# Two-layer graph network on one Trainium2 core: PSUM of the second linear map split into two groups of banks, two more pairs of half-batches in seven products, and the loads, copies and normalization steps around them reordered

## Chip, cores and metric

The kernel runs on one core of one Trainium2 chip, all in fp32. The metric is the device time of one execution in microseconds; a kernel's time is the median of its runs. Times inside an execution come from the hardware profiler.

## What is computed

The input is x of 16 batches (B) with 1024 nodes (N) and 256 channels (C), and one matrix adj of 1024x1024. In short:

```python
# layer 0
h = relu(layernorm(x))                              # per node
Wg = adj * A(column means of h)                     # a matrix per batch, from a sigmoid of differences
g = relu((h^T @ Wg) * para);  q = g^T in 4 heads
k, v = (h @ kv_w) in 4 heads
x = x + softmax(q k^T * scale) v
# layer 1
h = relu(layernorm(x))
agg = A_hat @ h                                     # A_hat from adj, once
z1 = agg @ W1^T + b1                                # 256 -> 512 (the first map)
h = relu(batchnorm(z1))                             # statistics over all 16*1024 nodes
z2 = h @ W2^T + b2                                  # 512 -> 256 (the second map)
x = x + batchnorm(z2)                               # again over all nodes
```

Both batch norms need their statistics over all nodes before anything behind them can start. So z1 is written to memory and read back, and z2 is kept in SBUF until it is complete.

## The kernel before

**Engines and order.** TensorE (PE in the profile) multiplies, VectorE (DVE) and ScalarE (ACT) do the element work and the copies out of PSUM, GpSimd (POOL) a few small steps and the turning of h by DMA, SyncE (SP) issues most loads and stores. Inside `tc.manual_schedule` the order of instructions on each engine is the order in which the program calls them; what an engine waits for follows from the tiles. A tile pool hands out buffers in turn; a request waits until the buffer's last reader is done. A DMA is issued by an engine's queue in order, so a load that waits for its buffer holds back the DMAs behind it on that queue.

**Stage 1** loops over the batches: attention of batch b, with the graph step of batch b+1 and the first map of earlier work placed between. `graph(b, between)` (L374) forms g, then queries, values (L423) and keys; at fixed places it calls the steps that the caller hands it in `between`. `between[7]` is `norm.relu(4, NC)`: `norm` is the layer-1 layer norm of the other batch, and its relu (L278) is done on ScalarE chunk by chunk, eight chunks of 128x256, each 0.505 us apart. Keys of b of 2 and more are formed as seven products of 2x2 blocks (Strassen's scheme in Winograd's form) with one PSUM bank `x` that goes on accumulating: after each step ScalarE copies it out (L474, L478, L482, L487). `between[8]` calls `leave` (stores x, L927) and `arrive(b + 2)`, which loads x of a coming batch on SyncE (L188) into the one buffer from which the relu reads.

`linear1` (L672) multiplies by A_hat (L690) in seven products, from four sums of parts of h that VectorE makes (L683 to L686); `linear1_seven` (L781) does the map W1 in seven products (L796), with `store` and `stats` (bn_stats, L835) of its results. Batches 14 and 15 run at the end of the stage (L1157 to L1189). There the step `third` turns W2 by TensorE into a PSUM tile of 128x1024 of the pool `ps_s` (L1027), and ScalarE copies it out (L1176).

**Stage 2** (from L1192) treats 32 half-batches t of 512 nodes. t of 31 and 30 and their z1 are the last to come out of stage 1, and their relus are done in place. A plain half-batch takes 8 matmuls of 128x512 (L1221): four pieces of 128 features, two output blocks c. `Pair(p)` (L1251) does the half-batches 2p and 2p+1 together in seven products of two matmuls (L1283), 14 in place of 16, in the order m1, m2, m6, m7, m5, m3, m4. m1, m6, m5 and m3 go on accumulating in the bank `x` (f_zx), which `keep` copies out by ScalarE after each (L1294); m2, m7 and m4 go to other banks (f_zm), which VectorE adds to z2 (L1297). VectorE makes the sums t1 to t4 of the relus (L1273, L1274, L1278, L1279). ScalarE applies the batch norm and relu of z1 in place (L152), after the loads (L163). m1 of pair p+1 stands between m5 and m3 of pair p.

All of these banks come from one pool `ps_z` of 8. The half-batches 0 and 1 are done plain at the start (begun with two of the four pieces, since those norms are ready first), the pairs 1 to 12 in seven products, the half-batches 26 to 29 plain, and 30 and 31 at the end in a pool `ps_last` of four banks (L1473). Plain results are copied to z2 by VectorE (L1349). Each result's statistics are a bn_stats on VectorE (L1234).

Then come the second batch norm and the **output** loop over b (L1512 to L1555): `finish` scales z2 (L1498 on ScalarE, L1500 on VectorE), TensorE turns it back (L1516, f_outps), VectorE adds it to x (L1549), and ScalarE's queue stores it (L1550). x is loaded again by `load_x1` (L1205) into tiles of the pool `io`, ten batches ahead at most. That pool also serves the loads of z1 for the pairs; it has 15 tiles of 512 KB.

Of the kernel before, what the change touches and what calls it, by code (L numbers as in the profile page):

```python
# [29 lines left out]
def fast_path(  # L30
# [140 lines left out]
    with ExitStack() as stage:  # L171
# [202 lines left out]
        def graph(b, between):  # L374
# [43 lines left out]
            def values():  # L418
                for c4 in range(0, NC, 4):
# [10 lines left out]
                    nc.scalar.copy(v[:, c4 : c4 + 4, :], ps)  # L430

            if b < 2:
                for d in range(CC):
                    ps = ps_s.tile([P, N], F32, tag="s", name=f"f_kps_{b}_{d}")
                    for g in range(NH):
                        for e in range(CC):
                            nc.tensor.matmul(
                                ps[:, ts(g, 512)],
                                kvw_t[:, e, ts(d, P)],
                                hT[e][:, ts(g, 512)],  # L440
                                start=(e == 0),
                                stop=(e == CC - 1),
                            )
                    nc.scalar.copy(kT[:, d, :], ps)
                    queries(d)
                values()
                return qT, kT, v
# [27 lines left out]
            mult(m2, a(0, 1), part(1, 0))  # L475
            nc.vector.tensor_add(c(0, 0), c(0, 0), m2)
            mult(x, sums[:, 1], t2, True)
            nc.scalar.copy(c(1, 0), x)  # L478
            mult(m7, sums[:, 2], t3)
            nc.vector.tensor_add(c(1, 0), c(1, 0), m7)  # L480
# [190 lines left out]

        def linear1(b, h1, thirds, between):  # L672


            def a(i, k):
                return h1[:, KH * k : KH * (k + 1), ts(i, P)]

            def pair_of_sums(n):
                return pp.tile([P, 2, KH, P], F32, tag="acc", name=f"f_hs{n}_{b}", bufs=2)

            s12, s34 = pair_of_sums(1), pair_of_sums(3)
            s1, s2, s3, s4 = s12[:, 0], s12[:, 1], s34[:, 0], s34[:, 1]
            nc.vector.tensor_add(s1, a(1, 0), a(1, 1))  # L683
            nc.vector.tensor_sub(s2, s1, a(0, 0))  # L684
            nc.vector.tensor_sub(s3, a(0, 0), a(1, 0))
            nc.vector.tensor_sub(s4, a(0, 1), s2)  # L686

            def product(ps, left, right, more=False):
# [91 lines left out]

        def linear1_seven(b, agg, sums, up, middle):  # L781

# [81 lines left out]
            add_biased(0, 1, m3)  # L864
            store(0, 1)
            stats(1, 1)
            stats(0, 1)
# [24 lines left out]

        def linear1_all(b, h1, thirds, early, late, last):

# [8 lines left out]
            def second(agg, up):  # L903
                if up is None:
                    up = ow.tile([P, 2, 512], F32, tag="oT", name=f"f_u4_{b}", bufs=2)
                linear1_seven(b, agg, sums[0], up, last)

# [14 lines left out]

            linear1(b, h1, thirds, [first, late, second if b + 1 < B else very_last])

# [105 lines left out]
        with tc.manual_schedule(engines={ENG.PE, ENG.Activation, ENG.DVE, ENG.Pool, ENG.SP}):  # L1030
# [73 lines left out]
            for b in range(B):  # L1104
# [14 lines left out]
                def more(c):  # L1119
# [12 lines left out]
                    6: [lambda: norm.relu(0, 4)],  # L1132
                    7: [lambda: norm.relu(4, NC)],
                    8: [lambda: leave(b), lambda: arrive(b + 2)],
# [25 lines left out]
                else:  # L1160
# [11 lines left out]
                    def third():  # L1172
                        left[5]()
                        norm.stats(4, NC)
                        norm.invert()
                        nc.scalar.copy(  # L1176
                            w2T.rearrange("p f c -> p (f c)"), turned(w2n, CC, FC, "w2")
                        )
                        norm.relu(0, NC)
# [7 lines left out]

                    linear1_all(b - 1, kept_h, thirds, first, second, third)
                    linear1_all(b, norm.h, thirds, nothing, nothing, nothing)  # L1189


    with ExitStack() as stage:  # L1192
        big = stage.enter_context(tc.tile_pool(name="fbig2", bufs=1))
        io = stage.enter_context(tc.tile_pool(name="fio", bufs=NH * (AHEAD - 3) + 1))

# [13 lines left out]
        with tc.manual_schedule(engines={ENG.PE, ENG.Activation, ENG.DVE, ENG.Pool, ENG.SP}):  # L1209
            bn1.affine(FC - 2, FC)  # L1210

            z2 = big.tile([P, CC, B - 1, N], F32, tag="z2", name="f_z2")
            zps = ExitStack()
            ps_z = zps.enter_context(tc.tile_pool(name="fps_z", bufs=8, space=PSUM))

            def bank(name):
                return ps_z.tile([P, 512], F32, tag="z", name=name)

# [30 lines left out]
            class Pair:  # L1249
# [5 lines left out]
                def load(self):  # L1255
# [7 lines left out]
                    self.b[0, 0] = fetch(t0, 0, new("b11"))  # L1263
                    self.b[1, 0] = fetch(t0, 2)
                    self.b[0, 1] = fetch(t1, 0, new("b12"))
                    self.b[1, 1] = fetch(t1, 2, new("b22"))
                    self.t4 = new("t4")

# [30 lines left out]
                def m1(self):  # L1299
                    self.x = bank(f"f_zx_{self.p}")  # L1300
                    self.mult(self.x, a(0, 0), self.b[0, 0], True)
# [45 lines left out]
            def plain_out(t, ps):  # L1347
                for c in range(CC):
                    nc.vector.tensor_copy(place(t, c), ps[c])  # L1349
                    stats(t, c)  # L1350

            SEVEN = range(1, B - 3)
            rest = range(2 * SEVEN[-1] + 2, TT - 2)

            def fetch_all(t):
                for f2 in range(0, FC, 2):
                    z = io.tile([P, 2, 512], F32, tag="x1", name=f"f_zz_{t}_{f2}")
                    zs[t, f2] = fetch(t, f2, z)

# [4 lines left out]
            pairs = {p: Pair(p) for p in SEVEN}  # L1364
            begun = {}
            for t in range(2):
                begun[t] = [bank(f"f_z2ps_{t}_{c}") for c in range(CC)]
                plain(t, begun[t], 0)
            weight_sums()
            for t in range(2):  # L1370
                relu_on(zs[t, 2], 2)
                plain(t, begun[t], 2)
            first = pairs[SEVEN[0]]
            first.load()
            for k, j in ((0, 0), (0, 1), (1, 1), (1, 0)):
# [8 lines left out]
            for p in SEVEN:  # L1384
                now, soon = pairs[p], pairs.get(p + 1)
                if p + 2 in pairs:
                    pairs[p + 2].load()
                now.m2()
                stats(now.t[0], 0)
                if soon:  # L1390
                    soon.relu(0, 0)
                    soon.relu(0, 1)
                now.m6()
                now.keep(0, 1)
                now.m7()
                if soon:
                    soon.relu(1, 1)
                    soon.relu(1, 0)
                now.m5()
                now.keep(1, 1)  # L1400
                if soon:
                    soon.sums13()
                    soon.m1()
                    soon.keep(0, 0)
                else:
                    for t in rest:
                        fetch_all(t)
                    for t in range(TT - 2, TT):
                        for f2 in range(0, FC, 2):
                            zs[t, f2] = fetch(t, f2)  # L1410
                    for n in range(AHEAD - 3):
                        load_x1(n)
                    ps = [bank(f"f_z2ps_{rest[0]}_{c}") for c in range(CC)]
                    relu_all(rest[0])
                    plain(rest[0], ps, 0)
                now.out(1)
# [12 lines left out]
            load_x1(AHEAD - 1, [(lasting, "w2n", 1), (io, "x1", None)])  # L1429
            for n, t in enumerate(rest):  # L1430
                if n == 0:
                    plain(t, ps, 2)
                else:
                    ps = [bank(f"f_z2ps_{t}_{c}") for c in range(CC)]
                    relu_all(t)
                    plain(t, ps, 0)
                    plain(t, ps, 2)
                plain_out(t, ps)
            zps.close()
            ps_out = stage.enter_context(tc.tile_pool(name="fps_out", bufs=2, space=PSUM))  # L1440
            ps_last = stage.enter_context(tc.tile_pool(name="fps_last", bufs=4, space=PSUM))
            last = {}
            for t in range(TT - 2, TT):
                relu_all(t)

# [14 lines left out]
            for c in range(CC):  # L1460
                for t in range(TT - 2, TT):
                    ps = ps_last.tile([P, 512], F32, tag="last", name=f"f_z2ps_{t}_{c}")
                    last[t % 2, c] = ps
# [31 lines left out]
            def scaled(out, src, c, by_scalar):  # L1495
# [3 lines left out]
                else:  # L1499
                    nc.vector.tensor_scalar(out, src, s, t, ALU.mult, ALU.add)  # L1500

            def by_scalar(b, c):
                return c == 0 or b % 2 == 1

# [15 lines left out]
            for b in range(B):  # L1520
# [6 lines left out]
                if b == 0:  # L1527

                    finish(0, 0)
                    finish(1, 0)  # L1530
                    for h in range(NH):
# [8 lines left out]
                else:  # L1540
                    for h in range(NH):
                        for c in range(CC):
                            turn_out(b, h, c, outs[h])
                soon = [(b + 2, c) for c in range(CC)] if b + 2 < B else []
                for n in soon:
                    if by_scalar(*n):
                        finish(*n)
                for h in range(NH):
                    nc.vector.tensor_add(xt[h], xt[h], outs[h])  # L1549
                    nc.scalar.dma_start(out_v[:, 4 * h : 4 * h + 4, :], xt[h])  # L1550
                for n in soon:
                    if not by_scalar(*n):
                        finish(*n)
                if b + AHEAD < B:
# [515 lines left out]
```

## Time and profile before

| | us |
|---|---|
| runs | 2447.23, 2447.41, 2450.25 (median 2447.41) |
| profiled execution | 2446.91 |
| its span | 2445.0 |
| VectorE busy | 1777.3 (73%) |
| ScalarE busy | 1316.7 (54%) |
| start of stage 2's first matmul | 2169.44 |
| start of the output's first transposition | 2377.93 |
| last transposition | 2433.24 |

The granted TensorE clock was 0.996 of full speed. In a line of the timeline the first number is the start in us from the beginning of the span, the second the length of a group of instructions; then follow the engine, the line in the kernel, the operation, its output and inputs by the program's names, and how many instructions the group has. Brackets give the idle time of the engine just before, and what ended it. In the list of waits, the numbers are the total, how often, and the longest.

### The profile page before, as it was taken

What the parts mean: (1) busy time and instruction counts of PE and PEld (TensorE: products, weight loads), DVE (VectorE), ACT (ScalarE), POOL (GpSimd) and SP (SyncE); (2) the same over time, 40 slices, a digit from 0 to 9 for tenths busy, and PEclk for the clock granted to TensorE, in tenths of its full rate; (3) what the DMA queues carried; (4) which work ended last, traced back from release to release, by engine and by line L of the source; (5) the groups of instructions that cost most, each with busy time, mean ns of one, the idle gap of its engine ahead of it and who ended that gap; (6) DMA issues with size and microseconds to landing.
All of it is one profiled execution on the core that took longest, in us unless ns stands there. A gap on an engine that the chain in (4) does not pass through costs nothing.

```text
span 2445.0 us, 24677 instructions
## 1 busy us (share of the span) xinstructions
PE 2390.1 (98%) x8050; PEld 1052.2 (43%) x8050; DVE 1777.3 (73%) x2440; ACT 1316.7 (54%) x1918; POOL 308.2 (13%) x546
## 2 busy tenths in 40 slices
PE   8999999999999999999999999999999999999995
PEld 4443444434343434344443434343444434434444
DVE  6878677685959596776859595958777687747746
ACT  6845556454636464654546364645546465346633
POOL 2030202020110303020202002030202020000000
PEclk9999999999999999999999999999999999999998
DMA  5041414232322424141422233241414211455569
GB/s 185 9 139 61 151 61 142 69 109 68 109 86 75 128 64 148 61 151 61 125 78 90 79 100 103 67 144 61 151 61 138 74 49 51 142 194 172 167 214 377
DMA packets 176632, 275.76 MB, mean 113 GB/s; under 512 B 37872, under 2 KB 121328, under 8 KB 176496
## 3 DMA queue, kind: packets, MB, share of 16 engines
q1 hardware_dynamic: 156336, 241.55, 30.6%
q0 software_dynamic: 15552, 15.77, 2.5%
q10 hardware_dynamic: 4608, 16.78, 1.7%
q8 instruction: 66, 1.08, 0.2%
q14 instruction: 70, 0.57, 0.1%
HBM read 169.35 MB, written 71.10 MB: 98 GB/s over the span
## 4 chain that ended last, share of the span: by engine, by line
PE 79%; DVE 11%; SPq 3%; DMA 3%; ACT 2%; issue 2%; POOL 1%; DVEq 0%; ACTq 0%; POOLq 0%
PE f_aps L690 15%; PE f_s L501 14%; PE f_o L542 14%; PE f_gps L398 13%; PE f_zps L796 5%; DVE f_acc L518 3%; PE f_vps L423 3%; PE f_zx L1283 3%; SPq L606 3%; PE f_zm L1283 2%; PE f_kpsx L464 2%; PE f_z2ps L1221 2%; PE f_kps L464 1%; ACT f_h_b L278 1%; DVE f_w L349 1%
## 5 line engine op out<-in xcount | busy, mean ns | idle before, releaser
L509 ACT ACTIVATE f_p<-f_s 128x1024 f32<-128x1024 f32 x512 | 477.3, 1048 | 153.4 <-PE f_s L501 153.3
L518 DVE TENSOR_TENSOR f_acc<-f_acc,f_p 128x1024 f32<-128x1024 f32 x384 | 470.4, 1225 | 41.1 <-ACT f_p L509 0.5
L501 PE MATMUL f_s<-f_qT,f_kT 64*128 64x512 f32 x2048 | 456.8, 596 | 0.0
L542 PE MATMUL f_o<-f_p,f_v 128*64 128x512 f32 x2048 | 453.6, 595 | 0.0
L398 PE MATMUL f_gps<-f_w,f_h_a 128*128 128x512 f32 x1024 | 444.7, 594 | 0.3 <-DVE f_w L336 0.3
L368 POOL DMA_DIRECT2D f_hT<-f_hQ x480 | 235.8, 499 | 1219.9 <-PE f_gps L398 1170.7
L501 PEld LDWEIGHTS f_s<-f_qT,f_kT 64*128 64x128 f32 x2048 | 190.7, 185 | 263.6 <-ACT f_p L509 117.3
L398 PEld LDWEIGHTS f_gps<-f_w,f_h_a 128*128 128x128 f32 x1024 | 192.8, 190 | 247.0 <-issue 229.8
L542 PEld LDWEIGHTS f_o<-f_p,f_v 128*64 128x64 f32 x2048 | 141.4, 137 | 304.3 <-issue 253.9
L349 DVE SCALAR_TENSOR_TENSOR f_w<-f_w,f_adj 128x1024 f32<-128x1024 f32 x127 | 153.8, 1212 | 38.8 <-ACT f_w L348 38.8
L345 ACT ACTIVATE f_w<-f_row,f_col 128x1024 f32<-128x1024 f32 x127 | 147.0, 1158 | 28.1 <-DMA f_row<-frow 18.7
L278 ACT ACTIVATE f_h_b<-f_x,f_shift_b,f_rstd_b 128x256 f32<-128x256 f32 x128 | 64.7, 587 | 161.0 <-DVE f_shift_b L263 161.0
L348 ACT ACTIVATE f_w<-f_w 128x1024 f32<-128x1024 f32 x127 | 134.3, 1058 | 4.0
L690 PE MATMUL f_aps<-f_ahatT,f_hs 128*128 128x512 f32 x256 | 115.1, 592 | 0.0
L690 PE MATMUL f_aps<-f_t,f_hs 128*128 128x512 f32 x256 | 112.5, 592 | 1.3 <-DVE f_hs L684 1.3
L423 PE MATMUL f_vps<-f_kvw,f_hT 128*128 128x256 f32 x512 | 113.1, 379 | 0.0
L690 PE MATMUL f_aps<-f_ahatT,f_h_b 128*128 128x512 f32 x256 | 112.6, 592 | 0.0
L278 ACT ACTIVATE f_h_a<-f_x,f_shift_a,f_rstd_a 128x256 f32<-128x256 f32 x126 | 73.8, 587 | 63.4 <-DVE f_shift_a L263 63.4
L423 PEld LDWEIGHTS f_vps<-f_kvw,f_hT 128*128 128x128 f32 x512 | 97.3, 190 | 20.1 <-issue 7.4
L515 DVE TENSOR_TENSOR f_acc<-f_p,f_p 128x1024 f32<-128x1024 f32 x64 | 76.2, 1191 | 15.3 <-ACT f_p L509 15.3
L584 ACT COPY f_recs<-f_rec 32x32 f32<-32x32 f32 x128 | 31.5, 246 | 98.6 <-DVE f_rec L576 97.5
L569 ACT COPY f_parts<-f_red 32x64 f32<-32x64 f32 x128 | 39.1, 305 | 78.4 <-DVE f_red L534 77.3
(230 smaller groups left out, 2694.8 us busy)
## 6 DMA issues: line engine op xcount, KB each, us to landing
f_t<-ft SPq DMA_DIRECT2D x84, 512.0 KB, 6.9
fz<-f_z SPq DMA_DIRECT2D x64, 512.0 KB, 9.7
f_x<-in_x_dram SPq DMA_DIRECT2D x31, 1024.0 KB, 7.8
f_zb<-fz SPq DMA_DIRECT2D x36, 512.0 KB, 4.2
f_para<-in_L_gnn_para_dram SPq DMA_DIRECT2D x32, 512.0 KB, 4.4
f_att<-f_oT SPq DMA_DIRECT2D x512, 32.0 KB, 1.9
fx<-f_x SPq DMA_DIRECT2D x16, 1024.0 KB, 6.5
f_x1t<-fx SPq DMA_DIRECT2D x32, 512.0 KB, 6.6
```

The lines of the kernel that those rows point to most:

```text
L278: nc.scalar.activation(self.h[:, c, :], self.xt[:, c, :], AF.Relu, bias=self.shift[:, c : c + 1], scale=self.rstd[:, c : c + 1], accum_out ...
L345: nc.scalar.activation(w, rows[b], AF.Abs, bias=cols[b][:, c : c + 1], scale=0.5 / C)
L348: nc.scalar.activation(w, w, AF.Tanh)
L349: nc.vector.scalar_tensor_tensor(w, w, 1.0, adj_t[c], ALU.subtract, ALU.mult)
L368: queue.dma_start(to[ts(k, 32), ts(a, 32 * NC)], t[ts(a, 32), k].rearrange("i c r -> i (c r)"),)
L398: nc.tensor.matmul(gps[d][:, ts(g, 512)], hs[b][:, c, ts(d, P)], w[:, ts(g, 512)], start=(c == 0), stop=(c == NC - 1),)
L423: nc.tensor.matmul(ps[:, i, :], hT[e][:, ts(c4 + i, P)], kvw_t[:, e, C : 2 * C], start=(e == 0), stop=(e == CC - 1),)
L501: nc.tensor.matmul(ps[:, e, :], kT[rows_e, pair, ts(m, P)], qT[rows_e, pair, ts(g, 512)], start=True, stop=True,)
L509: nc.scalar.activation(p, ps, AF.Exp)
L518: nc.vector.tensor_add(acc_of[s], acc_of[s], p)
L542: nc.tensor.matmul(o_of[s][e * HD : (e + 1) * HD, :], v[:, m, ts(2 * pair + e, HD)], p[:, e, :], start=(m == 0), stop=(m == NC - 1),)
L690: nc.tensor.matmul(ps, left[:, m, :], right(m), start=not more and m == 0, stop=(m == KH - 1), skip_group_check=more,)
```

## The change

1. In `graph`, the relus of chunks 4 to 7 leave `between[7]` and become two steps "late": for b of 2 and more, chunks 4 and 5 follow the key copy L474, 6 and 7 the copy L478. For b below 2 they precede the keys.
2. The sums of h for batch 15 are made in a function of their own, called ahead of the four statistics at the end of batch 14 (`ending`).
3. W2 is turned into two PSUM tiles of 128x512 of the pools `ps_o` and `ps_t`, with a ScalarE copy for each.
4. In stage 2, a pool `ps_x` of four banks takes f_zx and, at the end, the half-batches 30 and 31; `ps_z` keeps four banks for the other products and the half-batches 0 and 1. The pool `ps_last` is gone. `io` is allocated ahead of `big`, so its place in SBUF is another.
5. A pair's loads go in the order b11, b12, b22, b10, and the first pair's loads are called earlier.
6. The half-batches 0 and 1 are copied out by ScalarE.
7. Pairs 13 and 14 are done in seven products too, so that no plain half-batches remain in the middle. The loads of 30, 31 and x move into these two pairs, and the relus of 30 and 31 into pair 14.
8. In the output, block 0 of four batches (before: two) is scaled first, block 1 of batch 2 goes to ScalarE, and in the first round the further scaling follows the additions.

```diff
@@ graph @@
+            late = between.get("late", ())
             if b < 2:
+                for step in late:
+                    step()
...
             nc.vector.tensor_add(c(0, 0), c(0, 0), m2)
+            late[0]()
             mult(x, sums[:, 1], t2, True)
             nc.scalar.copy(c(1, 0), x)
+            late[1]()
@@ linear1_seven @@
             store(0, 1)
+            ending()
             stats(1, 1)
             stats(0, 1)
@@ stage 1 @@
-                    7: [lambda: norm.relu(4, NC)],
+                    "late": [lambda: norm.relu(4, 6), lambda: norm.relu(6, NC)],
...
-                        nc.scalar.copy(
-                            w2T.rearrange("p f c -> p (f c)"), turned(w2n, CC, FC, "w2")
-                        )
+                        for n, (pool, tag) in enumerate(((ps_o, "o"), (ps_t, "t"))):
+                            ps = pool.tile([P, 2, CC, P], F32, tag=tag, name=f"f_w2ps_{n}")
...
+                            nc.scalar.copy(
+                                w2T[:, 2 * n : 2 * n + 2, :].rearrange("p d c -> p (d c)"),
+                                ps.rearrange("p d f q -> p (d f q)"),
+                            )
...
+                        lambda: made.extend(sums_of_h(b, norm.h)),
@@ stage 2 @@
+        io = stage.enter_context(tc.tile_pool(name="fio", bufs=NH * (AHEAD - 3) + 1))
         big = stage.enter_context(tc.tile_pool(name="fbig2", bufs=1))
-        io = stage.enter_context(tc.tile_pool(name="fio", bufs=NH * (AHEAD - 3) + 1))
...
+            ps_x = stage.enter_context(tc.tile_pool(name="fps_x", bufs=4, space=PSUM))
             zps = ExitStack()
-            ps_z = zps.enter_context(tc.tile_pool(name="fps_z", bufs=8, space=PSUM))
+            ps_z = zps.enter_context(tc.tile_pool(name="fps_z", bufs=4, space=PSUM))
...
                     self.b[0, 0] = fetch(t0, 0, new("b11"))
-                    self.b[1, 0] = fetch(t0, 2)
                     self.b[0, 1] = fetch(t1, 0, new("b12"))
                     self.b[1, 1] = fetch(t1, 2, new("b22"))
+                    self.b[1, 0] = fetch(t0, 2)
...
-                    self.x = bank(f"f_zx_{self.p}")
+                    self.x = bank(f"f_zx_{self.p}", ps_x)
...
-                    nc.vector.tensor_copy(place(t, c), ps[c])
+                    nc.scalar.copy(place(t, c), ps[c])
...
-            SEVEN = range(1, B - 3)
+            SEVEN = range(1, B - 1)
...
                 if p + 2 in pairs:
                     pairs[p + 2].load()
+                elif p + 1 in pairs:
+                    for t, f2 in ((TT - 2, 0), (TT - 2, 2), (TT - 1, 0)):
+                        zs[t, f2] = fetch(t, f2)
+                    load_x1(0)
+                else:
+                    zs[TT - 1, 2] = fetch(TT - 1, 2)
+                    for n in range(1, AHEAD - 3):
+                        load_x1(n)
...
-                else:
-                    for t in rest:
-                        fetch_all(t)
...
-            for n, t in enumerate(rest):
...
-                plain_out(t, ps)
@@ output @@
+            EARLY = 4
+
             def by_scalar(b, c):
-                return c == 0 or b % 2 == 1
+                return c == 0 or b % 2 == 1 or 0 < b < EARLY
...
-                    finish(0, 0)
-                    finish(1, 0)
+                    for n in range(EARLY):
+                        finish(n, 0)
...
+                if b > 0:
+                    finish_soon(True)
                 for h in range(NH):
                     nc.vector.tensor_add(xt[h], xt[h], outs[h])
                     nc.scalar.dma_start(out_v[:, 4 * h : 4 * h + 4, :], xt[h])
-                for n in soon:
-                    if not by_scalar(*n):
-                        finish(*n)
+                if b == 0:
+                    finish_soon(True)
+                finish_soon(False)
```

## Prediction

> **What bounds the kernel now.** I read the engine table first: whether one engine carries the span decides what an edit is worth.
>
> ```profile
> PE 2390.1 (98%) x8050; PEld 1052.2 (43%) x8050; DVE 1777.3 (73%) x2440; ACT 1316.7 (54%) x1918; POOL 308.2 (13%) x546
> ```
>
> TensorE (PE) is busy for 2390.1 of 2445.0 us. So only two things shorten the kernel: fewer matmuls, or fewer of the holes left. The list of TensorE's waits (us in total, times, longest) names the holes; these are the ones that the change comes near:
>
> ```profile
> PE f_outps L1516 <- ACT f_z L1498: 12.5, 7, 6.4
> ...
> PE f_kpsx L464 <- ACT f_kT L474: 2.9, 4, 0.9
> PE f_zm L1283 <- DVE f_z L1297: 2.0, 1, 2.0
> ...
> PE f_zm L1283 <- ACT f_z L152: 1.4, 1, 1.4
> PE f_z2ps L1221 <- ACT f_z L886: 1.4, 1, 1.4
> PE f_z2ps L1221 <- ACT f_zz L152: 1.4, 1, 1.4
> PE f_zps L796 <- ACT f_w2T L1176: 1.4, 1, 1.4
> PE f_aps L690 <- DVE f_hs L684: 1.3, 1, 1.3
> PE f_zx L1283 <- DVE f_zt L1278: 1.2, 1, 1.2
> PE f_z2ps L1221 <- issue: 0.8, 1, 0.8
> ```
>
> The f_outps waits are the output stage, which moves data rather than multiplies. Its rows of the DMA view, 2320 to 2446 us in 40 slices of 3.15 us:
>
> ```profile
> DMA  8999997654444840165688999999999999999940
> GB/s 268 352 397 307 398 298 254 207 185 139 139 147 147 278 155 0 16 226 205 224 330 276 382 363 416 410 419 419 421 421 420 416 415 417 420 419 420 410 166 3
> ```
>
> From about 2389 us to the end it runs at some 418 GB/s: TensorE's holes there are free, and the stage ends when its bytes have moved. The timeline of TensorE gives the starts that the sums use:
>
> ```profile
> 2169.44 14.00 PE L1221 MATMUL f_z2ps<-f_z,f_w2T 128*128 128x512 f32 x32 [1.40 <-ACT f_z L886]
> 2183.28 1.88 PE L1283 MATMUL f_zx<-f_zb,f_w2T 128*128 128x512 f32 x4
> 2186.60 1.98 PE L1283 MATMUL f_zm<-f_z,f_w2T 128*128 128x512 f32 x4 [1.44 <-ACT f_z L152]
> 2189.77 1.96 PE L1283 MATMUL f_zx<-f_zt,f_w2s 128*128 128x512 f32 x4 [1.18 <-DVE f_zt L1278]
> ...
> 2200.57 1.98 PE L1283 MATMUL f_zm<-f_zt,f_w2T 128*128 128x512 f32 x4 [1.98 <-DVE f_z L1297]
> ```
>
> Undisturbed products follow each other every 1.717 us (four instructions, two matmuls), so one 128x512 matmul is 0.858 us. A bracket understates its hole by about 0.15 us: 2186.60 − 2183.28 − 1.717 = 1.60 against 1.44, as ends are modelled with an overhang. I count from start to start.
>
> **A. Keys (late relus).** From the first key matmul to the first L690 matmul takes 6.32 us in 10 of 14 batches, and 7.21, 7.37, 7.38 and 6.69 in four: 3.4 us too much in all. There ScalarE comes late to the copy L474, since its eight relus of 0.505 us stand ahead. Four of them now follow the copies L474 and L478. ScalarE's timeline in the batch at 550 us shows the room:
>
> ```profile
> 551.14 4.04 ACT L278 ACTIVATE f_h_b<-f_x,f_shift_b,f_rstd_b 128x256 f32<-128x256 f32 x8 [10.39 <-DVE f_shift_b L263]
> ...
> 558.83 0.59 ACT L474 COPY f_kT<-f_kpsx 128x512 f32<-128x512 f32 x1
> 560.63 0.59 ACT L478 COPY f_kT<-f_kpsx 128x512 f32<-128x512 f32 x1 [1.22 <-PE f_kpsx L464]
> 562.44 0.58 ACT L482 COPY f_kT<-f_kpsx 128x512 f32<-128x512 f32 x1 [1.22 <-PE f_kpsx L464]
> ```
>
> After L474 and after L478 it sits idle for 1.22 us; two relus take 1.01 and fit, with 0.2 to spare. ScalarE reaches L474 2.0 us sooner, more than the 1.06 of the worst batch: gain **3.4** (2 to 3.5, if a pair of relus makes a copy late). What is queued behind: the load of x for the batch after next (SyncE, L188), which overwrites what the relus read. In this batch it went at 555.21; it will go at about 562.3, and the w1s load (issued 562.43) behind it at about the same time as now. L188's loads land in 2.8 to 11.4 us, median 5.7, so at about 568; VectorE reads x at 571.78. Nothing in the median case; see the last rival.
>
> **B. W2 turned into resting banks, sums of h earlier.** Before: w2ps at 2120.92, zps at 2123.34, sixteen L690 instructions from 2128.59 (6.87 us), the next product at 2136.90. Without the transposes' copy ahead of it, zps runs on and L690 could start at 2127.1; but its bank comes free with the VectorE addition L852 at 2127.79, which sits behind a wait for GpSimd's rstd. So it starts at 2127.9, its two products end at 2134.8, and the sum s2 is there at about 2134.4, as four bn_stats (2.46 us) no longer precede it. Gain 2136.90 − 2134.8 = **2.1** (1.5 if the sums are late; 3.0 if both holes vanish). The 1.40 in front of f_z2ps stays: the first of these matmuls still waits for the last activation L886. **0**; 1.4 more if it goes.
>
> **C. Pools.** Two groups of four banks in place of eight in rotation. The Trainium skill ("Perfetto Trace Analysis", Matmul Optimizations) says to use all 8 PSUM banks for the most parallelism, which speaks against a split. The rows: in a steady pair a bank of m2 or m7 is read by the L1297 addition (0.68 us) within the pair, and the next claim of its bank comes two pairs (24 us) later; the x group's bank is claimed one pair (12 us) later, and its last copy is done within 2. By the row the split costs 0; by the rule, were each of 14 pairs to lose one hole of 1.0, it would cost 14. I take 0, except once, under E.
>
> **D. First pair.** Before: m2 at 2186.60 waits for the relus of b10, last loaded but one; m6 at 2189.77 for VectorE's sums; m4 at 2200.57 for the m2 addition at 2196.14, which lies behind four copies with statistics (2190.86 to 2196.10). Now b10 is loaded last, the loads go about 0.9 us earlier, and the four copies go to ScalarE (0.58 each, four in 2.0, ahead of the copy of m1's bank). b12 was issued at 2173.54 and landed 9.3 later; b12 and b22 will be issued at about 2172.3 and 2172.65, and b10 at 2173.1. With the landings moved by 0.9 only (the rate, not the issue, seems to set them) I estimate b12 in at 2180.7, b22 at 2182.1, b10 at 2183.2. Two relus take 1.5: b22's end at 2183.65, b10's at 2185.15. m2 waits for the first ScalarE copy of a bank, 2185.65: start 2185.75. The sums start near 2183.7; three operations of 1.23 and a handover put m6 at 2187.7. From there five products without a hole: m4 at 2187.7 + 5·1.717 = 2196.3. Gain **4.2** (1 if the loads land no earlier and ScalarE is late; 5.2, all three holes, at best).
>
> **E. End of the second map.** Before, t=26..29 took 16 plain matmuls per pair: two pairs in seven products save 2·2 = 4 matmuls, 4·0.858 = 3.43. The hole before f_zz (2331.32 − 2328.05 − 1.717 = 1.55) and the one marked issue (0.97 by starts: VectorE's copy out of t=29 frees the whole pool) go. New: in pair 14 no next m1 stands between m5 and m3, so m3 waits for ScalarE's copy of the same bank: 0.58 + two handovers, like the key copies, about 0.95; and t=31's last load, issued only at pair 14's m2, may push ScalarE's relu ahead of that copy, 0.5 more. 3.43 + 1.55 + 0.97 − 1.4 = **4.5** (3.3 to 5). Loads of x1 wait for pair 14's m6, m7, m5 and m3 (the last two for m4, about 2353): landed some 6 us or more before the output stage asks.
>
> **F. Output.** c=0 of four batches scaled first, (2,1) on ScalarE: the bytes stay the same and the DMA rate is full, so only the stage's start can gain: 0.3 (−1, if a scaling delays the first store at 2382.70; 0.7).
>
> Sum: 3.4 + 2.1 + 4.2 + 4.5 + 0.3 = **14.5 us**. The profiled execution took 2446.91, 1.9 around its span of 2445.0, so 2432.4 (span 2430.5); the median of the runs is 0.5 above, 2447.41: **2432.9**.
>
> **Rivals.**
> 1. *ScalarE becomes the bound of the first pair.* It gets the copies just where its relus end. For: it has no idle time from 2182.92 to 2190.56, and landings were 8 to 10 us there, with the rate only 116 to 260 GB/s. Against: VectorE's copies are what m4 waits for. Then D is 1 and A's small gaps leave 2: 14.5 − 3.2 − 1.4 = 9.9, **2437.5**.
> 2. *It doesn't do what it says.* Each wait is replaced by the next one: the bank wait of f_z2ps stays (shown by the order), the pool's waits return in pair 14. What remains is 3.43 for the matmuls, 2 for the keys and 0.6 of B: 6.0, **2441.4**. Against: the holes have different causes, and for A, B and D what is next is priced above.
> 3. *Slower: the x load comes too late.* Thirteen loads go 7.1 us later. VectorE's statistics at 571.78 would then wait, and through shift, eight relus (4.6 us on ScalarE) and the copy L742 so would TensorE, for which the slack is 1.5 + 0.5 us. TensorE loses once a landing takes over 9.5 + 2.0 = 11.5 us: the longest of L188's was 11.4. To turn the gain it must be 13.1 us on average in 13 batches, 13·1.6 = 20.8 us lost: 2447.4 − 14.5 + 20.8 = **2453.7**. For: the w1s load and turned h share the queues. Against: 5.7 median.
>
> **How the numbers follow.** The sum 0.64; rival 1 0.20; rival 2 0.08; rival 3 0.04; the rest, with losses and gains that cancel, 0.04. The range takes the high ends (3.5 + 3.0 + 1.4 + 5.2 + 5 = 18, 2429.4) and reaches up to rival 2 (2441.4): 2429.4 to 2441.5, of which the parts' low ends (2 + 1.5 + 1 + 3.3 − 1 = 6.8, 2440.6) are inside. 0.2% (4.9 us) is about what a measurement of this kernel can tell from no change: faster 0.90, same 0.05, slower 0.05.
>
> **What would show it.** A: all fourteen key stretches at 6.32, no wait for f_kT, L188 7 us later, no VectorE wait for x. B: no wait for w2T or hs before L690, but f_z2ps still waiting 1.4 for L886. D: from m2 to m4 of pair 1, 10.5 us instead of 13.97. E: one new TensorE wait of 1 to 1.4 for the bank copy in pair 14. F: from the first f_outps to the end of the span the same 67.1 us, at 418 GB/s. Wrong would make it: any wait by VectorE for f_x in the batches, a wait for z loads at each pair, or an output stage lengthened by 1.25 us (512 KB at 418 GB/s) for each x1 tile not yet there.

## The result

The kernel after takes 2432.46 us (median of 6 runs, 2431.01 to 2433.97), the kernel before 2447.30 (6 runs, 2442.22 to 2450.25): ratio 0.9943, 95% interval 0.993 to 0.9956. The forecast was 2432.9. The profiled execution took 2431.68, its span 2429.8, so 15.2 us less than the profiled one of before; the sum had said 14.5.

Where they came from is read off by starts of TensorE's instructions that both traces have (us; each row counts from the mark named in the row above it):

| from ... to | before | after | gain | forecast |
|---|---|---|---|---|
| start ... W2's turn (keys, A) | 2120.92 | 2117.48 | 3.44 | 3.4 |
| ... third and fourth products of L690/L703 (B) | 15.98 | 13.96 | 2.02 | 2.1 |
| ... first f_z2ps | 32.54 | 32.46 | 0.08 | 0 |
| ... m4 of pair 1 (D) | 31.13 | 25.86 | 5.27 | 4.2 |
| ... first f_outps (E) | 177.36 | 173.14 | 4.22 | 4.5 |
| ... end of the span (F) | 67.07 | 66.90 | 0.17 | 0.3 |

The list of TensorE's waits of the kernel after (total, times, longest) shows what is left:

```profile
PE f_outps L1534 <- ACT f_z L1514: 9.8, 5, 3.3
...
PE f_zx L1317 <- ACT f_z L1328: 1.8, 1, 1.8
PE f_z2ps L1255 <- ACT f_z L900: 1.4, 1, 1.4
PE f_aps L703 <- DVE f_z L865: 0.8, 1, 0.8
```

Gone are the waits for f_kT, for the relus L152, for the m2 addition, f_zt, f_w2T, f_hs and the one marked issue. The 1.4 before f_z2ps stands as forecast. Two lines have a new cause: 0.8 for the addition that frees L703's bank, and 1.8 for the bank copy in pair 14. The first pair in the timeline of TensorE, after:

```profile
2163.90 14.00 PE L1255 MATMUL f_z2ps<-f_z,f_w2T 128*128 128x512 f32 x32 [1.40 <-ACT f_z L900]
2177.74 1.88 PE L1317 MATMUL f_zx<-f_zb,f_w2T 128*128 128x512 f32 x4
2179.46 1.88 PE L1317 MATMUL f_zm<-f_z,f_w2T 128*128 128x512 f32 x4
2181.17 1.88 PE L1317 MATMUL f_zx<-f_zt,f_w2s 128*128 128x512 f32 x4
...
2189.76 1.88 PE L1317 MATMUL f_zm<-f_zt,f_w2T 128*128 128x512 f32 x4
```

No row behind the first has a bracket: m2 follows m1 by the undisturbed 1.72, and so does every product to m4. All three holes closed where I had left 0.98 us of two. The end of the map, TensorE and then ScalarE, after:

```profile
2341.17 1.88 PE L1317 MATMUL f_zx<-f_zb,f_w2s 128*128 128x512 f32 x4
2344.82 1.99 PE L1317 MATMUL f_zx<-f_zb,f_w2s 128*128 128x512 f32 x4 [1.77 <-ACT f_z L1328]
```

```profile
2342.78 1.52 ACT L152 ACTIVATE f_z<-f_z,f_bn_t,f_bn_s 128x512 f32<-128x512 f32 x2 [1.13 <-DMA f_z<-fz]
2344.20 0.56 ACT L1328 COPY f_z<-f_zx 128x512 f32<-128x512 f32 x1
```

The wait of m3 has the two parts that were named: the copy of the bank, and two relus ahead of it whose data landed only at 2342.78. In the nine variants below that have this hole its bracket is 1.1 to 1.4; 1.77 is the longest.

### The profile page after: what moved, and what is told of

The parts are those of the page before. It is cut to its first block, busy times and chain, and to the rows that moved or that the text cites. A ratio compares the mean times of both kernels' runs of the same rounds, so it can differ in the third digit from the quotient of the medians.

```text
span 2429.8 us, 24669 instructions
## 1 busy us (share of the span) xinstructions
PE 2387.0 (98%) x8042; PEld 1053.3 (43%) x8042; DVE 1781.9 (73%) x2441; ACT 1325.6 (55%) x1932; POOL 308.2 (13%) x546
## 4 chain that ended last, share of the span: by engine, by line
PE 96%; DMA 2%; DVE 1%; ACT 0%; issue 0%; SPq 0%; POOL 0%; DVEq 0%; ACTq 0%; POOLq 0%
PE f_s L506 19%; PE f_o L547 18%; PE f_gps L398 18%; PE f_aps L703 16%; PE f_zps L809 6%; PE f_vps L423 5%; PE f_zx L1317 4%; PE f_zm L1317 3%; PE f_kpsx L467 2%; PE f_kps L467 1%; DMA out_dram<-f_x1t 1%; PE f_z2ps L1255 1%; PE f_zps L891 1%; PE f_kps L440 1%; PE f_zps3a L809 0%; PE f_zps3b L809 0%
## 5 line engine op out<-in xcount | busy, mean ns | idle before, releaser
L278 ACT ACTIVATE f_h_b<-f_x,f_shift_b,f_rstd_b 128x256 f32<-128x256 f32 x128 | 67.8, 594 | 160.9 <-DVE f_shift_b L263 160.9
L703 PE MATMUL f_aps<-f_ahatT,f_hs 128*128 128x512 f32 x256 | 115.1, 592 | 0.0
L703 PE MATMUL f_aps<-f_ahatT,f_h_b 128*128 128x512 f32 x256 | 112.7, 593 | 0.8 <-DVE f_z L865 0.8
L703 PE MATMUL f_aps<-f_t,f_hs 128*128 128x512 f32 x256 | 112.5, 592 | 0.0
```

The lines of the kernel that those rows point to most:

```text
L703: nc.tensor.matmul(ps, left[:, m, :], right(m), start=not more and m == 0, stop=(m == KH - 1), skip_group_check=more,)
```

## Experiments

Each kernel is the kernel after with one thing changed, unless it says otherwise. TensorE's starts are the finer measure: four runs of one kernel lie 1 to 4 us apart. A *lead* below is the time from the start of VectorE's addition of f_att to x (L614, in the kernel after L619) to the first key matmul of the batch; a *stretch* runs from that matmul to the first L690/L703 matmul (L690 in before is L703 in after), and its *excess* is what it has over 6.32 us.

**late_back.** The relus go back to their old place:

```diff
-                    "late": [lambda: norm.relu(4, 6), lambda: norm.relu(6, NC)],
+                    7: [lambda: norm.relu(4, NC)],
...
-            late[0]()
...
-            late[1]()
```

> The kernel after, with the four relus of chunks 4 to 7 put back in their old place ahead of the queries and keys; all else as after. My theory: the key stretch (first key matmul to first L703 matmul) again lasts 7.2 to 7.4 us in three or four of the 14 batches and 6.32 in the others, a TensorE wait of about 2.9 us in all for the key copy is back, and the time is 3.4 us above the kernel after, about 2435.9. Rival (the keys gained from something else, or the late x load took part of the gain back): less than 1.5 us above, or more than 5.

2433.02 us (4 runs), W2's turn at 2116.47, no wait for f_kT in the list; thirteen of 14 key stretches at 6.32 and one at 6.42. The theory, as put, fell: the old place alone doesn't make the stretches long. The time, 0.6 above that of the kernel after, is where the rival had put it. What did is seen on VectorE. Its addition of f_att to x (L614) opens the chain statistics, rstd, shift, eight relus, and this is the one of before in the batch at 957 us, whose stretch is 7.21:

```profile
946.73 1.23 DVE L614 TENSOR_TENSOR f_x<-f_x,f_att 128x1024 f32<-128x1024 f32 x1 [4.66 <-DMA f_att<-f_oT]
```

It starts 10.82 us ahead of the first key matmul (957.55); in late_back, same batch, 11.72 ahead. Over the batches of before the lead and the excess go together: 10.82 and 0.90; 10.65 and 1.06; 11.34 and 0.38; with 11.86 or more it is nought, in all batches but one. So the excess is 11.7 less the lead, and what ends VectorE's wait is the landing of sixteen small DMAs. SyncE's rows of the batch at 957 us, in before and then in late_back, show one way in which they come late:

```profile
933.21 11.76 SPq L606 DMA_DIRECT2D f_att<-f_oT  x16
```

```profile
932.06 11.18 SPq L609 DMA_DIRECT2D f_att<-f_oT  x16
```

The first of the sixteen is issued 24.34 us ahead of the key matmul in both, but issuing them all takes 0.6 us longer in before (the usual length is 10.2). In the batch at 1626 us of before the issues take the usual 10.2 us, and the last DMA lands 3.99 behind its issue, where it takes 1.9 to 2.3 in the others.

The exception (lead 12.12, excess 1.05) is the batch at 1092 us; there GpSimd's queue shows a second way to the same end:

```profile
1076.90 5.86 POOL L368 DMA_DIRECT2D f_hT<-f_hQ  x12 [2.77 <-issue]
1083.84 0.50 POOL L368 DMA_DIRECT2D f_hT<-f_hQ  x1 [1.08 <-DMA f_hT<-f_hQ]
1084.36 1.66 POOL L257 TENSOR_TENSOR f_rstd_b<-f_var_b,f_mhalf 128x8 f32<-128x8 f32 x1
```

rstd has its input at 1082.76 and elsewhere starts 0.15 behind it; here it stands behind the last DMA of its own queue, which waited for another DMA, and starts 1.6 behind. Those 1.45 us taken off the lead (12.12 − 1.45 = 10.67) give 1.03, against the 1.05 found.

**slow_late and slow_back.** If a late landing is the cause, it can be given to every batch. One VectorE operation is put between landing and addition, in the kernel after (slow_late) and in late_back (slow_back):

```diff
                 def add():
+                    if g == 1 and b + 1 < B:
+                        again = kept["att"].rearrange("p r a h i -> p (r a h i)")
+                        nc.vector.tensor_tensor(again, again, again, ALU.max)
```

> The kernel after with one more VectorE operation of about 1.2 us per batch (a maximum of the tile f_att with itself, which leaves it as it is) between the landing of f_att and the addition L619 to x: as if that DMA landed 1.2 us later in every batch. The trace of the late_back run says that the four long key stretches of before were not there although the relus stood in the old place; they came where f_att landed about 1 us late. Theory margin: the late relus give ScalarE 2.0 us of room, so a landing later by 1.2 costs nothing: all key stretches at 6.32, time within 1 us of the kernel after (the operation itself is hidden). Rival: the late relus do nothing for it, and both kernels with the delay lose alike, 8 us or more.

> The same delay of 1.2 us per batch, with the relus in their old place (the kernel late_back with the operation added). Theory margin: without the late relus ScalarE has next to no room at the key copy, so most of the 13 or 14 key stretches grow from 6.32 to 7.0 to 7.6: 9 to 16 us above late_back, about 2445. Rival (the four stretches of before had another cause than the landing of f_att): under 3 us above late_back.

slow_late: 2432.53 us (4 runs), all stretches 6.31 or 6.32, though the leads fell to 9.91 to 11.61. slow_back: 2443.47 (20 runs), 10.9 above slow_late; in its profile all 14 stretches are long, 12.6 us in all, and its list of TensorE's waits has

```profile
PE f_kpsx L467 <- ACT f_kT L477: 10.8, 14, 1.6
```

Its leads and excesses keep to the same line in 13 of 14 batches: 9.99 and 1.72, 11.08 and 0.63, 11.40 and 0.31; the one off it, by 0.4, is again the batch near 1092 us. So what the late relus bring is a margin of at least 1.8 us against late data (a lead of 9.91 costs the stretch nothing), and what it is worth depends on how late the data come: 0.1 in late_back's profile, 12.6 in slow_back's.

The margin covers ScalarE's way alone. When rstd comes late on GpSimd, VectorE waits for it too, and the queries' operation (L415) stands behind that wait. In the batch near 1092 us this costs TensorE up to 1.0 us ahead of the keys, where the stretch doesn't show it, in four kernels that have the late relus (copies_back 0.3, slow_late 0.4, sums_back 0.7); the longest is in fill:

```profile
PE f_vps L423 <- DVE f_qT L415: 1.0, 1, 1.0
```

**before_again and late_alone.** What it is worth in the kernel before itself: a second profile of before, and before with only the late relus (the edit of late_back the other way round).

> The kernel before once more, for a second profile. The late_back run had the relus in the old place and one key stretch of 14 slightly long (6.42), where the first profile of before had four (3.4 us in all). Theory chance: how many stretches are long varies from one execution to the next with the landing of f_att, so this profile has another number than four, other batches, and their excess is anything from 0 to some 5 us. Rival (something in the kernel before fixes it): the same four batches, at 7.2, 7.4, 7.4 and 6.7.

> The kernel before with only the late relus of the change. All key stretches at 6.32. As the excess in before varies by execution, the gain of the median is what a typical execution loses: 3.4 us if the first profile was typical (about 2443), 0 to 1 if late_back was (about 2445.5). The other holes of before stay: 1.4 for w2T, 1.3 for hs, 4.6 in the first pair.

before_again (2445.86 us, one run): four long stretches, 3.2 us in all, at 290, 957, 1091 and 1625 us; three of them are batches of the first profile too. Neither theory as put: the batches are not drawn blindly, nor fixed. late_alone: 2444.01 (13 runs) against 2446.23 for before (17 runs), ratio 0.9991, interval 0.9983 to 1.0; no long stretch, though two of its leads are 10.76 and 11.19. So the median of before loses some 2.2 us to them (the interval reaches from nothing to 4.2), not the 3.4 of its first profile. That late_back had almost none fits a scatter between executions: eight profiles with the same instructions in this part of stage 1 (after, and seven variants that change only what comes later) give leads from 10.88 to 12.01 in the batch at 957 us and from 10.80 to 12.78 in the one at 1624; late_back has 11.72 and 12.72. Why it is mostly these batches that come late is open.

**order_back and place_back.** The first pair gained more than forecast. Its loads in the old order (b11, b10, b12, b22); and, apart from that, the pool io behind big again:

```diff
                     self.b[0, 0] = fetch(t0, 0, new("b11"))
+                    self.b[1, 0] = fetch(t0, 2)
                     self.b[0, 1] = fetch(t1, 0, new("b12"))
                     self.b[1, 1] = fetch(t1, 2, new("b22"))
-                    self.b[1, 0] = fetch(t0, 2)
```

> The kernel after, with each pair's loads in the old order b11, b10, b12, b22. The first pair gained 5.3 us where I had put 4.2: all its loads had landed sooner than I estimated. Theory order: the order of the loads made them land sooner (b10 second holds up the other two at the queue, and the stream is slower in that order): with the old order the holes before m2 and m6 of pair 1 return, 3.0 us together, time about 2435.4, and the DMA rate in the 5 us behind the first issue is near 200 GB/s. Theory place: the order is worth nothing by itself, the other place of the tiles in SBUF made the loads fast: no hole over 0.5 us, time within 0.5 us of the kernel after, rate over 300 GB/s.

> The kernel after, with the pool io allocated behind big again, so that its tiles lie where they lay before; order of loads as after. Theory order: nothing changes, time within 0.5 us of the kernel after. Theory place: the first pair's loads land 2 to 3 us later, their rate is near 200 GB/s, holes of 1 to 3 us before m2 and m6 of pair 1 return, time up to 2435.4. A third possibility: tiles that overlie others are held by their last readers, and the loads are issued later; then the issue times in SyncE's queue show it.

order_back: 2434.50 us (4 runs). TensorE's timeline has the hole before m2 again, and a small one of 0.27 by starts before m6:

```profile
2177.27 1.88 PE L1317 MATMUL f_zx<-f_zb,f_w2T 128*128 128x512 f32 x4
2180.32 1.98 PE L1317 MATMUL f_zm<-f_z,f_w2T 128*128 128x512 f32 x4 [1.18 <-ACT f_z L1383]
```

From f_z2ps to m4 it takes 27.54 us, 1.68 more than the kernel after: the order does matter, with half of the 3.0 forecast. The DMA view over 8 us from the first load's issue, in turn before, after and order_back:

```profile
DMA packets 419, 1.56 MB, mean 195 GB/s; under 512 B 38, under 2 KB 38, under 8 KB 419
```

```profile
DMA packets 666, 2.47 MB, mean 308 GB/s; under 512 B 64, under 2 KB 64, under 8 KB 666
```

```profile
DMA packets 483, 1.79 MB, mean 224 GB/s; under 512 B 46, under 2 KB 46, under 8 KB 483
```

These bytes are of all loads under way, nine to eleven in the 8 us, and not of the first four alone. With b10 second the view gives 195 to 224 GB/s in four profiles (before, before_again, late_alone, order_back), with b10 last 283 to 308 in ten. The fourth of the pair's loads has landed 10.7 to 12.0 us behind the first issue in the former, 8.0 to 9.2 in the latter. Nor does the order set a rate of its own: the rows of two stretches of before, 4 to 7 and 12 to 16 us behind the first issue, end in 145 and 423 GB/s, though pair 2's loads come in the same old order:

```profile
2176.16:2179.16 3.00, 3.00 (x8) 1.33 (x8) 0.00 (x0) 1.70 (x3) 0.00 (x0) 1.00 0.71 145
2184.16:2188.16 4.00, 2.56 (x7) 0.84 (x5) 2.25 (x2) 4.00 (x7) 0.00 (x0) 1.00 1.03 423
```

The same stretches are at 209 and 416 GB/s in order_back, 378 and 420 in the kernel after. So the loss is in one stretch at the start. The queue accounts for part: b10 waits for its buffer, so b12 is issued 1.4 us behind b11 instead of 0.4. One us doesn't explain the rest; what in the order does is open.

place_back: 2430.70 us (4 runs), 25.85 us from f_z2ps to m4, no hole, 287 GB/s in the same view. The place of the tiles is not the cause.

**copies_back.** The half-batches 0 and 1 copied out by VectorE again.

```diff
-                    nc.scalar.copy(place(t, c), ps[c])
+                    nc.vector.tensor_copy(place(t, c), ps[c])
```

> The kernel after, with the four copies of the half-batches 0 and 1 on VectorE again. By the rows of the kernel after VectorE ends the four sums at 2180.2, so the first copy ends at about 2181.0, and m2, whose bank it frees (the four banks of that group are all taken), starts at 2181.1 in place of 2179.46: a hole of 1.6 us. m4 then starts 1.6 later than in the kernel after anyway and needs the m7 bank's addition, which comes 9.6 us behind the sums as before, at 2189.8: no second hole. Time 1.6 us above the kernel after, about 2434.1. Rival, by which the copies held m4 alone: a hole of about 2 us before m4 and none before m2. Rival, by which the copies were harmless once the loads are early: under 0.5.

2433.35 us (4 runs), 27.53 us from f_z2ps to m4: 1.67 more, in one hole, at m2, as forecast, and none at m4:

```profile
2177.39 1.88 PE L1317 MATMUL f_zx<-f_zb,f_w2T 128*128 128x512 f32 x4
2180.70 1.96 PE L1317 MATMUL f_zm<-f_z,f_w2T 128*128 128x512 f32 x4 [1.43 <-ACT f_z L1328]
```

The bracket names a ScalarE copy, but that one was done at 2179.89. VectorE's first copy of a bank, which stands behind its four sums, ends at 2180.60, and m2, which needs that bank, starts 0.1 behind it:

```profile
2179.92 0.68 DVE L1383 COPY f_z<-f_z2ps 128x512 f32<-128x512 f32 x1
```

The label is an inference, and the times decide. In before the same copies cost at m4; with four banks for these products in place of eight they cost at m2.

**w2_back and sums_back.** The two edits of B, each undone alone (the edits are the diff's, turned round).

> The kernel after with W2 turned into the pool ps_s and copied out by one ScalarE copy, as before; the sums of h stay early. By the kernel after's rows, zps then waits 1.5 us, but L703 could not start before VectorE's addition L865 anyway (0.83 of wait in the kernel after): L703 starts 0.7 later and nothing else is late. Time 0.7 above the kernel after, about 2433.1. Rival, that the two edits' gains add: 1.4 to 1.5 above.

> The kernel after with the sums of h for batch 15 made behind the four statistics again; W2's turn as in the kernel after. The sum s2 then is ready about 2.5 us later, 2.0 after TensorE wants it: a wait of L703 for f_hs of 1.8 to 2.0 is back, all that both edits gained together. Time 2.0 above the kernel after, about 2434.4; so the turn of W2 alone would be worth nothing. Rival: the gains add, 1.3 above.

In the kernel after, L703 waits for the addition that frees its bank:

```profile
2124.49 7.11 PE L703 MATMUL f_aps<-f_ahatT,f_h_b 128*128 128x512 f32 x16 [0.83 <-DVE f_z L865]
2131.44 7.03 PE L703 MATMUL f_aps<-f_t,f_hs 128*128 128x512 f32 x16
```

w2_back: 2432.03 us (4 runs). Its wait for the copy is there in full, and counted from W2's turn L703 starts all the same only 0.66 us later, since it lost its wait for L865:

```profile
2119.78 1.98 PE L809 MATMUL f_zps<-f_zt,f_w1T 128*128 128x512 f32 x4 [1.39 <-ACT f_w2T L1192]
...
2125.03 7.03 PE L703 MATMUL f_aps<-f_ahatT,f_h_b 128*128 128x512 f32 x16
2131.90 7.03 PE L703 MATMUL f_aps<-f_t,f_hs 128*128 128x512 f32 x16
```

From W2's turn to the product with f_hs: 14.54 us against 13.96, so 0.6 (the median doesn't resolve that). sums_back: 2434.85 us (4 runs), 15.98 us on the same way, all that both edits had gained:

```profile
2133.47 7.11 PE L703 MATMUL f_aps<-f_t,f_hs 128*128 128x512 f32 x16 [1.86 <-DVE f_hs L688]
```

So the turn alone (sums_back) is worth nothing, the sums alone (w2_back) 1.4, both 2.0.

**early_back.** `EARLY = 2` in place of 4.

> The kernel after with two in place of four batches scaled first in the output, and block 1 of batch 2 on VectorE again. The stage moves its bytes at some 418 GB/s either way, so its length from the first transposition to the end of the span stays at 66.9 us within 1: time within 1 us of the kernel after. Rival (the early scaling carries the stage): 2 us or more above.

2431.84 us (4 runs). The output took 68.45 us in its profile, outside the 66.9 within 1 that was expected; but in the thirteen other profiles, of kernels before and after, it took 66.9 to 69.1. The edit's effect isn't told apart from that.

**fill.** A version that closes the hole in pair 14: four matmuls of half-batch 30 between m5 and m3, and the late relu behind the copy. The four matmuls are left out in their old place, behind m4; of the edit only the main part is shown.

```diff
+                else:
+                    early = bank(f"f_z2ps_{TT - 2}_0", ps_x)
+                    product(early, TT - 2, 0, 0)
+                    product(early, TT - 2, 0, 2)
+                    relu_on(zs[TT - 1, 2], 2)
                 now.out(1)
                 now.m3()
```

> The kernel after with the hole of pair 14 filled: the four instructions pairs of half-batch 30, block 0 (four matmuls, 3.43 us) stand between m5 and m3 of pair 14 in place of behind m4, and the relu of the last z1 tile of half-batch 31 follows the copy of the bank. The hole of 1.9 us before m3 goes, nothing else moves: 1.9 us below the kernel after, about 2430.5. If the output stage waits for the loads of x instead (they start when m7, m5 and m3 of pair 14 release their tiles, which m3 and m4 now do 1.5 us later against the end of the map), up to all of that is given back there.

```profile
2342.03 1.88 PE L1317 MATMUL f_zx<-f_zb,f_w2s 128*128 128x512 f32 x4
2343.75 3.60 PE L1255 MATMUL f_z2ps<-f_z,f_w2T 128*128 128x512 f32 x8
2347.18 1.88 PE L1317 MATMUL f_zx<-f_zb,f_w2s 128*128 128x512 f32 x4
```

The hole is gone: from W2's turn to the first f_outps it takes 243.39 us against 245.42. But the hole of the kernel after was the longest of its kind: from m4 to the first f_outps fill takes 171.1 us, and the nine other variants 172.5 to 172.7, so 1.5 is the fairer figure. The output took 67.57 (66.90), within its scatter. 2431.26 us (5 runs), ratio to before 0.9935, interval 0.9922 to 0.9949: 1.2 us under the kernel after's median, in another set of runs, and the two intervals overlap. The gain in the whole time is not shown.

## Why the prediction held, step by step

- **A, keys.** The size held in the two executions that were compared (3.44), the mechanism only in part. The room of 2.0 us and its price of nothing stood slow_late's test. But "there ScalarE comes late since its eight relus stand ahead" took four stretches of one execution as a constant of the kernel: they stand ahead in all batches, and a stretch grows where f_att or rstd comes late. The median of before loses some 2.2.
- **Rival 3.** SyncE issued x at 561.94 instead of 555.21, as worked out. VectorE's wait for x (f_st_a) is 4.2 us in two places, against 4.1 in two before, all within the first 8 us of the program; no batch lost anything. The loads that were moved landed in 5.4 to 5.7 us in before and 5.4 to 6.8 after: the 11.4 of the prediction is that of another load of the same line, so this rival was weaker than it looked.
- **B.** Right, by its own chain: L703's bank came free at the VectorE addition, 0.8 of wait, and s2 was there in time.
- **C.** No steady pair shows a wait for a bank, so splitting the eight banks cost 0 there. The sentence of the Trainium skill ("Perfetto Trace Analysis", Matmul Optimizations), which asks that all eight banks be in use, doesn't speak against the split: both kernels use all eight. Only at the start did the group of four matter, where it held back m2 in copies_back. One reading was too narrow: with one claim per pair and four banks, a bank of the x group is claimed again after four pairs, not one, so there was more room than priced.
- **D.** The mis-sized term: "the landings moved by 0.9 only (the rate, not the issue, seems to set them)". The issues came within 0.4 us of what was put, but counted from f_z2ps's start b12, b22 and b10 landed at 7.9, 9.4 and 10.7 us where the prediction has 11.3, 12.7 and 13.8. One reading of before was wrong too: b10 was not last loaded but one but second, and had landed at 2181.45. Its relus were late because they stand behind those of b12 and b22, and ScalarE waited for b12:

```profile
2182.92 2.93 ACT L152 ACTIVATE f_zb<-f_zb,f_bn_t,f_bn_s 128x512 f32<-128x512 f32 x4 [5.05 <-DMA f_zb<-fz]
2185.75 1.50 ACT L152 ACTIVATE f_z<-f_z,f_bn_t,f_bn_s 128x512 f32<-128x512 f32 x2
```

  In the kernel after, ScalarE has no such wait, and b10's relus end at 2176.55, 12.65 us behind f_z2ps's start, where I had put 15.7:

```profile
2170.82 4.32 ACT L152 ACTIVATE f_zb<-f_zb,f_bn_t,f_bn_s 128x512 f32<-128x512 f32 x6
2175.05 1.50 ACT L152 ACTIVATE f_z<-f_z,f_bn_t,f_bn_s 128x512 f32<-128x512 f32 x2
```

  So all three holes closed, the 5.2 that the prediction gave as the best case. Order and copies are worth 1.7 each when undone alone; the other 1.9 comes back with neither, and no run undoes both. Calling the loads earlier did little: b11 is issued 2.64 us behind f_z2ps's start, 2.72 in before.
- **E.** The matmuls and the two old holes went as summed; the new hole was 1.93 by starts where I had put 1.4. In the nine other profiles of this hole the bracket is 1.1 to 1.4, by starts about 0.16 more, which is my figure.
- **F.** The output's 66.9 us is its 67.1 of before: it moves its bytes. The gain of 0.17 is not told apart from nothing, since the output takes 67.0 to 67.8 in three profiles with the old output and 66.9 to 69.1 in ten with the new.

What is left over between 14.5 and 15.2 is D's surplus less E's shortfall. Against the medians the gain is 14.8; with the median of before in the later sets of runs (2446.07 to 2446.25), it is about 14. That the total came within half a us of the forecast is in part luck: A was priced at 3.4 where the medians of before and late_alone differ by 2.2, D was put too low, and the scatter of E and F in single profiles is as large as what they missed by.

## What to carry to other kernels

A wait that shows in some iterations and not in others marks a margin near zero: look for the late datum upstream, and price the edit as margin, by delaying that datum on purpose in both versions, not by the sum of one trace. Edits on one chain don't add: undo each alone before crediting it (here 0.0 and 1.4 made 2.0). In a chain that keeps one accumulator, a step that loses the independent work between two uses of it pays for the copy out (1.3 to 1.9 us here); other matmuls that are ready belong in that gap.

## What was not expected of the hardware

Nine to eleven loads of 512 KB were under way in the first 8 us of stage 2's stream. They moved at 195 to 224 GB/s where b10 stood second (four profiles) and at 283 to 308 where it stood last (ten), while 12 us behind the first issue both orders ran at some 420; where the tiles lay in SBUF made no difference. GpSimd's small operation lost 1.45 us behind DMA issues in its own queue. And the sixteen small DMAs of f_att landed up to 1.2 us late in some batches, often but not always the same ones.
